# Masked attention, 16 batches on one core: the products that number batch 2's tokens move behind a query and a value product, and the tail scores wait for fewer exponentials

## The chip, the core and the metric

The kernel runs on one core of a Trainium2 chip. The metric is the device time of one execution in microseconds. TensorE (PE), VectorE (DVE), ScalarE (ACT), GpSimd (POOL) and SyncE (SP, which here only issues transfers) each work through a queue of their own in order; they meet through semaphores.

## The reference

`x` is 16 x 512 x 1024 (batch, feature, token), `cond` a 0/1 mask of 16 x 1024, `Wq` and `Wo` are 512 x 512.

```
xt = transpose(x)                         # tokens x features
q = xt @ Wq.T ; qh = q in 8 heads of 64
scores = (qh @ qh.T) / 8                  # queries = keys = values
logits = (scores * cmask + (1 - cmask) * -1e30) * rmask
out = (softmax(logits) @ qh) @ Wo.T
return x + transpose(out)
```

A token whose mask is 0 sees equal logits everywhere, so all such tokens of a batch get the mean of all values. A token whose mask is 1 attends only to tokens whose mask is 1.

## The kernel before

About half the tokens of a batch are active. The kernel numbers the active tokens of each batch (`slots`), gathers their rows (`gather`), and does the whole attention on a compact batch of A = 544, 528 or 512 tokens. Batches 2 to 15 are taken in order of their count of active tokens, which the kernel works out itself (`order`, `permute`). Rows of inactive tokens get the mean's row added (`rest`).

The work of a batch b, in the names of the code:

- `slots`: counting products on PE (L245, L247, L250: triangular and all-ones matrices against the mask), then a chain of small VectorE steps (L251 to L274) that gives each token its place and makes one-hot rows `oht`. It is done for groups of batches; for batches 2 and 3 during batch 0.
- `hot` (L319) and `index` (L328): one-hot products that place token numbers, eight small matmuls, and the copy L331 that makes `idx`, the list for the gathers (`take`, L416 on POOL).
- `xt`: transposes of the gathered rows (L507), split into two f16 parts on ACT (L465) and DVE (L466); `xt(..., 4)` is for the tail tokens beyond 512.
- `query(e, g)`: for each of four head pairs e and two column halves g, 12 f16 products (L534), copied out by ACT (L538); `qsplit` splits q into f16 parts and four transfers on SP (L562 to L565) spread them into `xx`.
- `value(e)`: products that transpose q (L588 in batch 0, L591 after it), copied by ACT (L595); `tail_copy` and `value_tail` (L604, L617) do so for the tail tokens; `range_x` is a check on magnitudes.
- `scores(b, p, u)`: 16 products (L751) for head pair p, half u, into five banks of one PSUM tile, then four exponentials on ACT (L766), in the order of places 3, 0, 1, 2. Place k takes columns 40 + 544k to 584 + 544k (for A = 544), so places 0 and 1 cover banks 0 to 2, places 2 and 3 cover banks 2 to 4. The next scores wait for all four.
- `tail_scores(b, g)`: 16 products (L698) for the scores whose keys are the tail tokens of four heads, into banks 0 and 1 of the same tile, one exponential (L702), a split on DVE (L707, L708) and four transfers on SP (L714, L715).
- `attend` (L786) and `attend_tail` (L804): the context, copied out by ACT (L809); `recip`, `norm` (L890 to L898) scale it; `project` (L908) multiplies by Wo, L914 adds x and L995 scatters the rows.

While batch b is in its scores and contexts, the steps that prepare batch b + 1 (queries, values) and b + 2 (numbers, gathers) fill PE between them. From batch 1 on, PE's order is written out by hand in `plan`. In batch 0 there is no such plan: the steps stand in a list `m` with a cost each, they are emitted between the scores in proportion to these costs, and a list scheduler decides the order of the instructions of each engine from priorities, dependencies and its own cost model. The splits of Wo (`split`, casts L183 on ACT and L184 on DVE) are inserted into `m` behind `index`, at every third place.

The scheduler sees the PSUM tile as one buffer. `other_banks` declares that an instruction does not depend on another; `self.left` holds the exponentials of the last scores in the order they were issued, that is places 3, 0, 1, 2.

Of the kernel before, what the change touches and what calls it, by code (L numbers as in the profile page):

```python
# [47 lines left out]
class Fast:  # L48
# [637 lines left out]
    def tail_scores(self, b, p):  # L686


        nc, s = self.nc, self.st[b]
        A = s["A"]  # L690
        CH = A // 2
        if True:
            pt = self.ps[:, 0:2]
            for a in range(2):
                for g in range(2):
                    for r in range(HG):
                        xx, k = s["xx"][2 * p + r // 2], r % 2
                        self.beat = nc.tensor.matmul(pt[r * CT:(r + 1) * CT, g, :CH], lhsT=xx[:, 2 * k, 512:C],  # L698
                                                     rhs=xx[:, 2 * k + a, g * CH:(g + 1) * CH],
                                                     start=(a == 0), stop=(a == 1)).ins  # L700
            t = self.sb([P, C], F32, "p", 12)[:, :A]
            self.left.append(nc.scalar.activation(t.rearrange("p (g c) -> p g c", g=2), pt[:, :, :CH], AF.Exp,  # L702
                                                  bias=s["nm"][p][:, HG:], scale=SCALE, accum_out=s["zt"][:, p:p + 1]).ins)

            hi = self.sb([P, C], F32R, "c", 4)[:, :A]
            lo = t.bitcast(F32R)
            nc.vector.tensor_copy(hi, t)  # L707
            nc.vector.tensor_tensor(lo, t, hi.bitcast(F32), ALU.subtract)  # L708

            def spread():  # L710
                s["pt"] = self.sb([P, 2, C], F32R, "pt")[:, :, :A]
                half = slice(0, DK), slice(DK, P)
                for k in range(2):
                    nc.sync.dma_start(out=s["pt"][half[k], k, :].bitcast(F32), in_=hi[half[k]].bitcast(F32))  # L714
                    nc.sync.dma_start(out=s["pt"][half[1 - k], k, :].bitcast(F32), in_=lo[half[k]].bitcast(F32))  # L715

            self.later(spread)
# [318 lines left out]
    def run(self, flag):  # L1036
# [7 lines left out]
        def xt(n):  # L1044
            return [(0.45, L(self.xt, n, c)) for c in range(4)] + [(0.25, L(self.xt, n, 4))]

        def query(n, e, g):
            u = [(1.37, L(self.query, n, e, g))]
            return u + [(0, L(self.qsplit, n, e))] if g else u

        def value(n, e):
            return [(0.45, L(self.value, n, e))]
# [91 lines left out]
        if True:  # L1144
            stack = ExitStack()
            for b in range(B + 1):
# [22 lines left out]
                if n < B:  # L1169
                    q, x, v = (lambda e, g: query(n, e, g)), xt(n)[2 if b == 0 else 0:], (lambda e: [(0.25, L(self.value, n, e))])  # L1170
                    tc, tv = ((lambda g, f=f, c=c: [(c, L(f, n, g))]) for f, c in ((self.tail_copy, 0), (self.value_tail, 0.25)))
                    rng = [(0, L(self.range_x, n, c)) for c in range(DC)]
                    ahead = b + 2 < B
                    hot, index = ([(c, L(f, b + 2))] if ahead else [] for f, c in ((self.hot, 0), (self.index, 0.2)))
                    take = [(0, L(self.gather, b + 2, j)) for j in range(5 if self.wide[b + 2] > 512 else 4)] if ahead else []
                    if self.wide[n] == 512:
                        tc = tv = lambda g: []
                    if b:
                        pre = [(0, L(self.active, *g)) for g in new[0]]
                        post = [(0.3, L(self.slots, *g)) for g in new[0]] + [(0, L(self.facts_sums, *g)) for g in new[1]]  # L1180
                        end = [(0.1, L(self.facts_end, *g)) for g in new[1]]
                        plan = {(0, 0): sums + x[:2], (0, 1): x[2:4],
                                (3, 0): rows + x[4:] + q(0, 0) + second, (3, 1): pre + q(0, 1) + carry, (4, 0): value(b, 3),
                                (5, 1): vt(b, 1) + pk(b, 1), (6, 0): post,
                                (7, 0): third + q(1, 0) + tp(b, 1), (7, 1): q(1, 1) + P_(0) + bt(b, 1), (8, 0): tc(0) + v(0) + end + rng[:2],
                                (10, 0): tv(0) + tail + q(2, 0), (11, 0): hot + rng[2:],
                                (12, 0): q(2, 1), (12, 1): index + P_(1) + v(1), (13, 0): take[:3],
                                (14, 1): rest + pk(n, 0), (16, 0): P_(2) + take[3:], (16, 1): q(3, 0) + tp(n, 0) + q(3, 1),
                                (17, 0): bt(n, 0) + v(2) + tc(1) + [(0, L(self.means, n))]}
                        carry = P_(3)  # L1190
                    else:
                        m = sums + x + pk(b, 1)
                        for g in new[0]:
                            m += [(0, permute), (0, L(self.active, *g))]
                        m += q(0, 0) + tp(b, 1) + bt(b, 1) + q(0, 1)
                        for g in new[0]:
                            m += [(0.3, L(self.slots, *g))]
                        m += hot + q(1, 0) + index + q(1, 1) + take
                        m += rng[:2] + tc(0) + v(0) + tv(0) + rng[2:] + q(2, 0) + v(1)
                        m += q(2, 1) + pk(n, 0) + tp(n, 0) + q(3, 0) + bt(n, 0)  # L1200
                        m += q(3, 1) + v(2) + tc(1) + [(0, L(self.means, n))]
                    if b == 0:
                        k = next(k for k, (c, f) in enumerate(m) if f is index[0][1])
                        for c in range(DC):
                            m.insert(k + 1 + 3 * c, (0, L(self.split, "o", c)))
                else:

                    places = [("xi", 8), ("xa", 13)]
                    come = [[L(self.late, x, j, *places[k % 2]) for j in range(5, 9)] for k, x in enumerate(rests[b])]
                    leave = [[L(self.rest, x, j) for j in range(5, 9)] for x in rests[b]]  # L1210
                    free[0] = come[0]
                    for c, l in zip(come[1:] + [[]], leave):
                        free[0] += c + l
                    plan = {(0, 0): sums, (1, 1): second, (3, 0): rows + carry + value(b, 3) + pk(b, 1),
                            (3, 1): [(0, L(self.project_means, b))], (7, 0): third + tp(b, 1) + P_(0) + bt(b, 1), (11, 0): P_(1), (13, 0): P_(2), (14, 1): [(0, self.ranges)],
                            (16, 1): P_(3)}
                if b in (1, 2):
                    plan[12, 1] += [(0, L(self.range_w, " oq"[b], c)) for c in range(DC)]
                if b == 0:
                    m = begin + m  # L1220
# [204 lines left out]
```

## Time and profile before

| | us |
|---|---|
| median of 3 runs | 1013.18 |
| lowest, highest | 1012.51, 1014.59 |
| the profiled execution | 1017.15 |
| its span (first to last instruction) | 1015.4 |

The profile is of one execution of its own, slower than the three runs. In its rows, a time at the left is the start in microseconds from the start of the span, then follow the duration, the engine, the line of the code, the operation, what is written and read, the shapes, and how many instructions were merged. A bracket at the end gives the idle time of that engine just before, and what ended it. Rows of waits read: who waited, for whom; microseconds in total, times, the longest. `ACTIVATION_READ_ACCUMULATOR` is the part of an exponential that reads the row sums out.

### The profile page before, as it was taken

The page shows a single profiled execution, that of the slowest core. Times are in us where ns is not written, and L with a number is a line of the kernel's source. Part 1 is how long each engine was busy: PE and PEld are TensorE (multiplying, and loading weights), DVE is VectorE, ACT ScalarE, POOL GpSimd, SP SyncE. Part 2 cuts the span into 40 slices and gives each one's busy share as a digit, 9 for nine tenths or more (in the row PEclk, how much of TensorE's full clock was granted, in tenths as well). Part 3 has the DMA queues.
Part 4 walks back from the last instruction along what each step waited for, and adds up shares of the span by engine and source line. Part 5 has one row for each costly group of instructions (what it writes and reads, how often), then busy time and mean ns, then how long its engine had stood idle before and what let it go on. Part 6 is the DMA issues. An engine that isn't in the chain of part 4 may idle for free. (4 is left out here: it accounts for less than half of the span.)

```text
span 1015.4 us, 23009 instructions
## 1 busy us (share of the span) xinstructions
PE 956.1 (94%) x8236; PEld 593.1 (58%) x8236; DVE 718.4 (71%) x2413; ACT 656.6 (65%) x1696; POOL 312.1 (31%) x307
## 2 busy tenths in 40 slices
PE   7788999999999999999999999999999989999887
PEld 4455666656666656666666666666666656555333
DVE  7786775767776677787777788767678866665463
ACT  5766766657667666776767677676757766555441
POOL 3101013124131322415143241515224140424752
PEclk9999999999999999999999999999999999999989
DMA  6836555557556566756657675666667564645642
GB/s 212 231 106 183 123 151 162 163 163 210 135 173 171 154 180 192 206 155 198 182 173 215 209 198 160 194 175 177 199 209 208 157 184 137 178 122 182 215 161 99
DMA packets 78793, 177.69 MB, mean 175 GB/s; under 512 B 14688, under 2 KB 20576, under 8 KB 78672
## 3 DMA queue, kind: packets, MB, share of 16 engines
q1 hardware_dynamic: 57584, 108.40, 38.5%
q0 software_dynamic: 21088, 67.75, 21.2%
q8 instruction: 67, 1.10, 0.5%
q14 instruction: 54, 0.44, 0.1%
HBM read 91.49 MB, written 33.91 MB: 123 GB/s over the span
## 5 line engine op out<-in xcount | busy, mean ns | idle before, releaser
L766 ACT ACTIVATE p<-pss,nm 128x528 f32<-128x528 f32 (+2 forms) x512 | 354.6, 703 | 108.7 <-PE pss L751 83.0
L786 PE MATMUL pss<-p,v 128*64 128x264 f32 (+2 forms) x2048 | 244.3, 391 | 0.9 <-issue 0.9
L751 PE MATMUL pss<-xx 128*128 128x86 f16 (+31 forms) x1920 | 219.8, 288 | 4.1 <-ACT c L809 2.6
L995 POOL DMA_INDIRECT y_out<-xa,idx x68 | 84.5, 1243 | 425.5 <-DVE nm L664 91.7
L786 PEld LDWEIGHTS pss<-p,v 128*64 128x64 f32 x2048 | 141.6, 137 | 88.6 <-issue 10.2
L751 PEld LDWEIGHTS <-xx 128*128 128x128 f16 (+1 forms) x1920 | 108.6, 97 | 87.6 <-issue 35.6
L534 PE MATMUL pm<-xh,wqh 128*128 128x264 f16 (+5 forms) x512 | 143.0, 279 | 7.7 <-DVE xl L466 4.2
L534 PE MATMUL pm<-xh,wql 128*128 128x264 f16 (+5 forms) x512 | 142.5, 278 | 0.0
L534 PE MATMUL pm<-xl,wqh 128*128 128x264 f16 (+5 forms) x512 | 142.4, 278 | 0.1
L534 PEld LDWEIGHTS <-wqh 128*128 128x128 f16 x1024 | 97.4, 98 | 37.0 <-issue 17.8
L416 POOL DMA_INDIRECT xa<-x_in,idx x68 | 71.6, 1054 | 129.2 <-ACT q L538 51.4
L766 ACT ACTIVATION_READ_ACCUMULATOR p<-pss,nm 128x1 f32 x512 | 105.2, 205 | 0.0
L908 PE MATMUL pm<-woh,ch 128*128 128x512 f16 x240 | 92.5, 385 | 9.4 <-ACT q L538 5.1
L538 ACT ACTIVATE q<-pm 128x264 f32<-128x264 f32 (+5 forms) x128 | 50.8, 397 | 67.1 <-PE pm L534 42.4
L908 PE MATMUL pm<-wol,ch 128*128 128x512 f16 x240 | 92.4, 385 | 0.0
L908 PE MATMUL pm<-woh,cl 128*128 128x512 f16 x240 | 92.1, 384 | 0.0
L908 PEld LDWEIGHTS <-ch 128*128 128x128 f16 x480 | 45.2, 99 | 59.8 <-issue 12.9
L995 POOL DMA_INDIRECT y_out<-xi,idx x60 | 67.7, 1128 | 38.2 <-PE pss L698 17.7
L914 DVE SCALAR_TENSOR_TENSOR xa<-pm,xa 128x512 f32<-128x512 f32 x61 | 41.6, 683 | 52.9 <-PE pm L908 52.3
L416 POOL DMA_INDIRECT xi<-x_in,idx x60 | 62.1, 1034 | 35.1 <-PE pm L534 16.5
L809 ACT COPY c<-pss 128x528 f32<-128x528 f32 (+2 forms) x64 | 38.2, 597 | 50.0 <-PE pss L804 15.2
L595 ACT COPY v<-pm 128x512 f32<-128x512 f32 x64 | 37.5, 586 | 45.8 <-PE pm L591 44.8
(241 smaller groups left out, 1504.8 us busy)
## 6 DMA issues: line engine op xcount, KB each, us to landing
xx<-hl SPq DMA_DIRECT2D x224, 136.0 KB
xm<-x_nat_in SPq DMA_DIRECT2D x56, 512.0 KB
rb<-rd SPq DMA_DIRECT2D x72, 132.0 KB
rb<-rd SPq DMA_DIRECT2D x40, 136.0 KB
pt<-c SPq DMA_DIRECT2D x36, 132.0 KB
pt<-p SPq DMA_DIRECT2D x36, 132.0 KB
ub<-ud SPq DMA_DIRECT2D x16, 256.0 KB
xx<-hl SPq DMA_DIRECT2D x32, 128.0 KB
```

What stands on the lines that cost most here:

```text
L416: dma = self.nc.gpsimd.indirect_dma_start(out=tile[:n], out_offset=None, in_=self.x, in_offset=bass.IndirectOffsetOnAxis(ap=idx, axis=0))
L534: self.beat = nc.tensor.matmul(pq, lhsT=w[:, c, e * P:(e + 1) * P], rhs=xx[:, c, cols], start=(k == 0), stop=(k == 3 * DC - 1)).ins
L538: nc.scalar.activation(s["q"][:, e, cols], pq, AF.Copy, scale=1.0 / (SX * SW))
L595: nc.scalar.copy(v, pv)
L751: m = nc.tensor.matmul(flat[:, c0:c1], lhsT=w, rhs=x, start=banks[n] not in banks[:n], stop=banks[n] not in banks[n + 1:])
L766: e = nc.scalar.activation(t, flat[:, at:at + A], AF.Exp, bias=s["nm"][p // 2][:, p % 2 * 2 + k:p % 2 * 2 + k + 1], scale=SCALE, accum_out ...
L786: mm = nc.tensor.matmul(pav[k * DK:(k + 1) * DK, g], lhsT=s["v"][p][:, i, k * DK:(k + 1) * DK], rhs=ps[k, i][:, cols], start=(i == 3), sto ...
L809: self.context_out = nc.scalar.copy(c[:, :A].rearrange("p (g c) -> p g c", g=2), pav).ins
L908: mm = nc.tensor.matmul(po[:cols.stop - cols.start], lhsT=a[:, e, cols], rhs=w[:, e, :], start=(e == 0 and k == 0), stop=(e == DC - 1 and ...
L914: return self.nc.vector.scalar_tensor_tensor(x, po, 1.0 / (SX * SW), x, ALU.mult, ALU.add).ins
L995: dma = self.nc.gpsimd.indirect_dma_start(out=self.out, out_offset=bass.IndirectOffsetOnAxis(ap=idx, axis=0), in_=x, in_offset=None)
```

## The change

Two edits. In batch 0's list, `index` and `take` of batch 2 (the products that place token numbers, and the gathers that use them) go behind the second half of query product 1, the tail copy and value product 0 of batch 1. The splits of Wo, which are inserted relative to `index`, go with them in the list. And each product of the tail scores is declared independent of `self.left[0]` and `self.left[3]`, the exponentials of places 3 and 2, whose columns lie in banks 2 to 4; it remains tied to those of places 0 and 1.

```
                         self.beat = nc.tensor.matmul(pt[r * CT:(r + 1) * CT, g, :CH], lhsT=xx[:, 2 * k, 512:C],
                                                      rhs=xx[:, 2 * k + a, g * CH:(g + 1) * CH],
                                                      start=(a == 0), stop=(a == 1)).ins
+                        self.other_banks(self.beat, self.left[0], self.left[3])
...
-                        m += hot + q(1, 0) + index + q(1, 1) + take
-                        m += rng[:2] + tc(0) + v(0) + tv(0) + rng[2:] + q(2, 0) + v(1)
+                        m += hot + q(1, 0) + q(1, 1) + tc(0) + v(0) + index + take
+                        m += rng[:2] + tv(0) + rng[2:] + q(2, 0) + v(1)
```

In the built program the number of instructions on PE, DVE, ACT and SP that do work is the same. Their order differs only in the stretch of batch 0 that the prediction walks through; in the later batches the orders are the same, and the first of each tail scores' products waits for the third of the four exponentials instead of the fourth. The line numbers here and in the prediction are those of the kernel before.

## The prediction

> **What bounds the kernel now.** I read the page first, then busy time by stretches of 100 us, then what TensorE waited for.
>
> ```profile
> span 1015.4 us, 23009 instructions
> ...
> PE 956.1 (94%) x8236; PEld 593.1 (58%) x8236; DVE 718.4 (71%) x2413; ACT 656.6 (65%) x1696; POOL 312.1 (31%) x307
> ...
> 0.00:100.00 100.00, 79.12 (x649) 49.37 (x650) 75.42 (x255) 64.80 (x168) 17.43 (x38) 0.95 0.62 182
> ...
> 600.00:700.00 100.00, 98.39 (x904) 62.52 (x901) 75.62 (x274) 69.79 (x180) 29.72 (x25) 1.00 0.64 185
> ...
> PE pm L328 <- DVE oht L274: 3.3, 1, 3.3
> ...
> PE pss L698 <- ACT p L766: 3.0, 1, 3.0
> ```
>
> PE is the bound: in the middle it is busy 98 of 100 us, so a microsecond saved on it early moves everything behind it. The first 100 us are the hole: 79 us busy, and a granted clock of 0.95. Two of the long waits there are on lines that the change touches: the index products of batch 2 (L328) wait for VectorE, and the first tail scores (L698) for an exponential. L698 has this wait once in 28 tail scores: in the others the context product ahead of them outlasts the exponentials, so the second edit is worth nothing after batch 0.
>
> An idle PE also loses its clock afterwards. These are stretches cut where the clock changes (columns: length, then PE, PEld, DVE, ACT, POOL busy, granted clock, DMA share):
>
> ```profile
> 42.21:45.62 3.41, 1.10 (x19) 0.68 (x19) 3.41 (x5) 3.41 (x11) 0.00 (x0) 1.00 0.66 186
> 45.62:49.04 3.42, 3.42 (x20) 1.63 (x20) 3.41 (x7) 2.56 (x10) 0.00 (x0) 0.50 0.70 182
> 55.86:59.28 3.42, 1.50 (x11) 0.86 (x9) 3.42 (x9) 3.38 (x10) 0.00 (x0) 1.00 0.49 154
> 59.28:62.69 3.41, 3.38 (x21) 1.79 (x20) 3.41 (x14) 3.10 (x8) 0.00 (x0) 0.50 0.02 5
> 76.34:79.76 3.42, 0.78 (x13) 0.70 (x14) 3.28 (x17) 2.63 (x7) 0.00 (x0) 1.00 0.87 202
> 79.76:83.17 3.41, 3.41 (x18) 2.06 (x16) 1.94 (x12) 0.81 (x2) 0.81 (x1) 0.50 0.95 295
> ...
> 38.80:42.21 3.41, 1.68 (x17) 0.98 (x15) 0.72 (x3) 2.47 (x7) 0.00 (x0) 1.00 1.03 258
> ```
>
> Each time PE was busy 1.50 us or less of 3.41, the next 3.41 us ran at half clock; after 1.68 us busy (the last row) they did not.
>
> **Part 1: the first tail scores.** The second edit lets them start after the third of four exponentials.
>
> ```profile
> 41.88 0.73 ACT L766 ACTIVATE p<-pss,nm 128x544 f32<-128x544 f32 x1
> ...
> 42.57 0.74 ACT L766 ACTIVATE p<-pss,nm 128x544 f32<-128x544 f32 x1
> ...
> 43.87 0.66 ACT L446 ACTIVATE xi<-xi 128x512 f32<-128x512 f32 x1
> ...
> 44.49 0.74 ACT L702 ACTIVATE p<-pss,nm 128x544 f32<-128x544 f32 x1
> ...
> 43.45 0.85 PE L698 MATMUL pss<-xx 128*32 128x272 f16 x16 [2.98 <-ACT p L766]
> 45.37 2.90 PE L751 MATMUL pss<-xx 128*128 128x472 f16 x16 [1.06 <-ACT p L702]
> ```
>
> They start 42.57 - 41.88 = 0.69 earlier, at 42.76, and end at 43.6. In the built order the tail exponential (L702) takes the place of the sum at 43.87, so it starts 44.49 - 43.87 = 0.6 earlier, and so do the next scores: 44.8 instead of 45.37. I do not expect this 0.6 to last. On ACT the built order puts a value copy and three casts of Wo (L183) ahead of the next exponentials, and on PE the transposes of the tail tokens (L507 from xt) go from a gap before the scores to behind the context product:
>
> ```profile
> 54.70 1.26 ACT L183 ACTIVATE woh<-xa 128x512 f16<-128x512 f32 x2 [0.35 <-DMA xa<-wo_in]
> 55.87 0.70 ACT L766 ACTIVATE p<-pss,nm 128x544 f32<-128x544 f32 x1
> ...
> 59.26 0.63 PE L507 MATMUL pm<-ident,xt 32*128 32x32 f32 x4
> 59.92 3.00 PE L751 MATMUL pss<-xx 128*128 128x472 f16 x16
> ...
> 64.84 0.29 PE L534 MATMUL pm<-xh,wqh 128*128 128x272 f16 x1
> ...
> 66.24 0.27 PE L651 MATMUL pm<-ident,smcol 128*128 128x128 f32 x1
> ```
>
> The four exponentials from 55.87 on would start some 0.5 later (one more cast, 1.26/2 = 0.63, and the value copy, less the 0.35 of waiting and what came earlier), near 56.4. But nothing lies between them any more, so at 0.69 each they end at 56.4 + 4 x 0.69 + 0.1, and the scores of 59.92 start near 59.3. PE idles as long before them, so the half-clock stretch at 59.28 stays; some 0.2 of the 0.6 goes into it, and the tail transposes, now uncovered, cost 0.4. At the query product of 64.84 I take 0. Bounds: 0.6 saved, or 0.6 lost if the casts wait longer for Wo.
>
> **Part 2: the slots.** Their 16 counting products (L245 to L250) come behind the tail scores and the tail's context product, no longer ahead of them.
>
> ```profile
> 72.48 0.29 PE L534 MATMUL pm<-xh,wqh 128*128 128x272 f16 x1
> ...
> 72.95 1.71 PE L751 MATMUL pss<-xx 128*128 128x472 f16 x16
> ...
> 72.11 0.15 DVE L251 COPY n<-pm 128x2 f32<-128x2 f32 x1
> ...
> 78.70 0.37 DVE L274 TENSOR_TENSOR oht<-c,tok 128x72 f16<-128x72 f16 x2
> ```
>
> The same products end by 72.48 in either order, but the query product then waits for the copy L251, which now follows the last of them: 0.15 and a handover of some 0.1. It starts at 72.75, 0.3 late. Query products follow each other at (66.24 - 64.84)/12 = 0.117; three instead of four lie ahead of the end of the scores, so these end at 74.8 instead of 72.95 + 1.71 = 74.66: 0.15 lost. VectorE's chain from L251 to L274 moves by 0.6, its end from 79.07 to 79.7.
>
> **Part 3: the stall.** L328 waits for that chain, and a query product, a value product and the next scores are queued behind it on PE.
>
> ```profile
> 78.98 0.36 PE L328 MATMUL pm<-oht,tmp 128*128 128x9 f16 x8 [3.29 <-DVE oht L274]
> ...
> 81.46 2.54 PE L751 MATMUL pss<-xx 128*128 128x472 f16 x16
> 83.92 3.89 PE L786 MATMUL pss<-p,v 128*64 128x272 f32 x32
> ...
> 88.35 0.38 PE L591 MATMUL pm<-two,xx 128*128 128x64 f16 x7
> ...
> 74.76 0.72 ACT L766 ACTIVATE p<-pss,nm 128x544 f32<-128x544 f32 x1 [1.40 <-PE pss L751]
> ...
> 77.71 0.22 ACT L766 ACTIVATION_READ_ACCUMULATOR p<-pss,nm 128x1 f32 x1
> ```
>
> Without it, 9 + 12 query products (21 x 0.117 = 2.4) and one value product (0.1) follow the scores' end, and PE is ready at 77.3. Late next are the exponentials that free the scores' banks: they took from 74.76 to 77.93, 3.17, and start 0.1 after the scores, so they end at 78.1. That is a new wait of 0.75, too short to lose the clock. The scores then take 1.71, as in the row of 72.95, and the context product starts at 79.85 instead of 83.92: 4.1 saved. Check by pieces: the wait 3.29 goes; so does the half clock (78.98 to 81.46 is 2.48 for work of 0.2 + 1.40 + 0.1, and the scores took 2.46 instead of 1.71: 1.5), and the eight index products (0.2); 0.15 and 0.75 are paid.
>
> On the clock: the Trainium skill, page "TensorE: Matmul & The Clock Gate", section "Part 1: The HAM clock gate", gives windows of 3413 ns and lets the clock fall after a window in which PE idles. The window's length agrees with the rows above; the condition does not, since 1.50 us of work in 3.41 did not keep the clock. By that rule a stall of 3.29 us alone would cost no clock.
>
> **Part 4: the moved products, and the end.** L328 now stands behind the rest of value product 0, at 79.85 + (88.35 - 83.92) + 0.3 = 84.6, 4.9 after VectorE is done with the chain: no wait, 0.2 of work. Its copy L331 waits on VectorE behind the norm of head pair 1, and L617, which is behind L328 and the scores on PE, needs L331. The gathers of batch 2 follow L331.
>
> ```profile
> 86.28 0.24 DVE L898 TENSOR_TENSOR ctl<-c,cth 128x32 f16<-128x32 f32 x1
> ...
> 8.99 1.13 POOL L416 DMA_INDIRECT xa<-x_in,idx  x1 [5.58 <-DVE later L191]
> ...
> 13.30 0.63 PE L507 MATMUL pss<-ident,xa 128*128 128x128 f32 x4 [1.56 <-DMA xa<-x_in,idx]
> ...
> 102.83 0.63 PE L507 MATMUL pm<-ident,xa 128*128 128x128 f32 x4
> ```
>
> The norm ended at 86.52 and has no reason to be later; L617 is due at 84.8 + 1.71 = 86.5. The first gather needed 13.30 - 8.99 = 4.3 from issue to use, so batch 2's lands near 91 and is read at 102.83 - 3.9 = 98.9: covered by 8 us. On SP's queue a load of x goes behind four spreads of q; its sum comes much later. From about 95 us on all engines have the old order, so the saving is carried to the end: 4.1 less 0.2, **3.9 us**.
>
> The profiled execution took 1017.15, of which 1015.4 are the span; less 3.9 that is 1013.25. It was 3.97 above the median of the three runs, 1013.18, whose work and order are the same, so I carry the difference: **1009.3 us**. About 0.2%, 2 us, is what a measurement of this kernel can tell from no change.
>
> **The rivals.** (a) The stall loses no clock in ordinary runs (the rule above): then 1.5 was never there to save, 2.4 is left, 1010.8. For it: how stretches fall on the stall may differ by run. Against it: three low stretches here, three losses.
> (b) PE is busy over 1.6 us in the stretch before 59.28 and keeps its clock: 3.00 - 1.71 = 1.3 more, 1008.0. Against it: PE waits as long as before.
> (c) The casts of Wo become the bound. They now stand ahead of the exponentials of 55.87, and SP issues Wo's loads behind four transfers of the tail exponentials (L714, L715). In the row of 54.70 a cast waited for its load, so the cover is thin. Each microsecond that the third cast passes 56.4 is lost on PE; at 2 to 4 us the gain is gone: about 1012.5. (d) The same at 4.5 us, where PE idles long enough for a further half-clock stretch (1.5): 4.5 + 1.5 - 3.9 = 2.1 slower, 1015.3; from there on the change is a loss. Against both: DMA is at 0.70 and 0.49 in those stretches, not full.
> (e) The stall is not removed but moves with L328, because VectorE's chain ends later than 84.6. Against it: 4.9 us of slack. I count it with (c).
>
> **How the numbers follow.** Forecast 0.62, (a) 0.13, (b) 0.07, (c) with (e) 0.12, (d) 0.06. Of (a), 0.08 is past 2 us. Faster by over 0.2%: 0.62 + 0.08 + 0.07 = 0.77; within 0.2%: 0.05 + 0.12 = 0.17; slower: 0.06. Range: below, (b) with the 0.6 of Part 1 and 1.2 for the spread of a median (the three runs lie 2.08 apart): 1006.2; above, (c) at 1012.6. It leaves out (d) and the ends of the others.
>
> **What would show it.** Right: no wait at L328, no half clock near 80 us, a wait of about 0.7 for the exponentials at the second scores after the slots, L698 held only by the third exponential, and the scores of 59.92 at about 59.3. Wrong: a long wait of L751 or L786 between 55 and 62 us with L183 late on ACT, or L617 waiting for L331.

## The result and the profile after

The changed kernel took 1010.68 us (median of 20 runs, 1006.18 to 1016.64), the kernel before 1016.17 in the 20 runs beside it: a ratio of 0.9935, 95% interval 0.9914 to 0.9957. The ratio is not that of the two medians, which is 0.9946. It was timed twice more: 1008.85 against 1013.91 (0.9961, 0.9929 to 0.9994) and 1008.67 against 1015.12 (0.9936, 0.9907 to 0.9966). So it is faster, by 4.0 to 6.6 us by the ratios and by 5.1 to 6.5 by the medians; the prediction's 3.9 us is a ratio of 0.9962.

Its page, and the two stretches of 100 us that were shown of before (length; PE, PEld, DVE, ACT, POOL busy; granted clock; DMA share and rate). One line was added at 701, so the lines behind it are one higher than before: L751 is now L752, L766 is L767, L786 is L787.

```profile
span 1004.5 us, 23007 instructions
...
PE 951.6 (95%) x8236; PEld 592.2 (59%) x8236; DVE 716.7 (71%) x2413; ACT 656.6 (65%) x1696; POOL 314.5 (31%) x307
...
0.00:100.00 100.00, 80.67 (x672) 51.28 (x672) 76.72 (x267) 68.60 (x179) 18.12 (x38) 0.95 0.66 188
600.00:700.00 100.00, 97.68 (x894) 62.14 (x890) 74.93 (x274) 69.32 (x180) 30.01 (x27) 1.00 0.61 177
```

The first 100 us hold 1.5 us more of PE's work, the middle is nearly as full as before (97.7 us of 100, for 98.4). The timeline of PE in the changed kernel answers the walk row by row:

```profile
42.11 0.85 PE L698 MATMUL pss<-xx 128*32 128x272 f16 x16 [2.28 <-ACT p L767]
...
59.29 1.72 PE L752 MATMUL pss<-xx 128*128 128x472 f16 x16 [1.40 <-ACT p L767]
...
71.30 0.28 PE L534 MATMUL pm<-xh,wqh 128*128 128x272 f16 x1 [0.25 <-DVE n L251]
...
76.68 1.72 PE L752 MATMUL pss<-xx 128*128 128x472 f16 x16 [0.75 <-ACT p L767]
78.33 3.89 PE L787 MATMUL pss<-p,v 128*64 128x272 f32 x32
...
82.97 0.35 PE L328 MATMUL pm<-oht,tmp 128*128 128x9 f16 x8
83.18 1.70 PE L752 MATMUL pss<-xx 128*128 128x472 f16 x16
...
93.44 0.30 PE L651 MATMUL pm<-ident,smcol 128*128 128x128 f32 x1 [2.58 <-DVE smcol L645]
```

L328 has no wait, the exponentials hold PE for 0.75 us, the copy L251 for 0.25. These three were forecast. The last row was not: the transpose of the peaks (L651) now waits 2.58 us. In before the same row reads, with the gathers and the query's copy that belong to it:

```profile
82.36 0.95 POOL L416 DMA_INDIRECT xa<-x_in,idx  x1 [46.86 <-ACT q L538]
...
87.55 0.87 POOL L416 DMA_INDIRECT xt<-x_in,idx  x1 [0.30 <-issue]
...
96.28 0.42 ACT L538 ACTIVATE q<-pm 128x274 f32<-128x274 f32 x1
...
97.82 0.30 PE L651 MATMUL pm<-ident,smcol 128*128 128x128 f32 x1 [0.46 <-DVE smcol L645]
```

and in the changed kernel:

```profile
84.63 0.95 POOL L416 DMA_INDIRECT xa<-x_in,idx  x1 [49.76 <-ACT v L595]
...
89.84 1.22 POOL L416 DMA_INDIRECT xt<-x_in,idx  x1 [0.30 <-issue]
...
88.80 0.28 PE L534 MATMUL pm<-xh,wqh 128*128 128x274 f16 x1
89.15 1.71 PE L752 MATMUL pss<-xx 128*128 128x472 f16 x16
...
91.98 0.40 ACT L538 ACTIVATE q<-pm 128x274 f32<-128x274 f32 x1 [1.34 <-PE pss L752]
```

PE's rows end its query product at about 89.3 and the scores behind it at 90.9, yet ScalarE, which has nothing else to do from 90.64 on, copies that product only at 91.98. The fifth of five gathers that GpSimd issues back to back ends at 89.84 + 1.22 = 91.06. VectorE's chain to `smcol` stands behind that copy in VectorE's order, and L651 needs the chain.

To follow the saving, this table gives the start of the same instructions of PE in each profile, less that in before (us; negative is earlier). The heads are before's times: a query product, the second scores after the slots, two later scores, and L651 between them. From 111 us on the orders are those of before. The profile of e12 is from another chip than the others.

| profile | 64.84 | 72.95 | 95.65 | L651, 97.82 | 111.37 |
|---|---|---|---|---|---|
| changed | -1.56 | -1.43 | -6.50 | -4.38 | -1.95 |
| changed, second (e4) | -0.99 | -0.92 | -5.99 | -3.73 | -3.65 |
| changed, third (e10) | -0.19 | -0.06 | -5.14 | -3.03 | -0.58 |
| before again (e11) | 1.49 | 1.48 | 1.41 | 1.42 | 1.44 |
| list alone (e1) | 0.59 | 0.58 | -4.60 | -2.66 | -2.59 |
| ties alone (e2) | -0.02 | 0.04 | 0.68 | 3.15 | 1.21 |
| products in the wait (e3) | -0.57 | 0.11 | -0.84 | -0.84 | -0.83 |
| gathers twice (e5) | 1.16 | 1.23 | -3.84 | -0.25 | 4.33 |
| plain transfers (e6) | -0.08 | -0.02 | -5.09 | -5.09 | -2.84 |
| slots early (e7) | 0.82 | 1.16 | -2.50 | -2.49 | -2.49 |
| slots early, ties (e8) | 1.38 | 1.52 | -1.60 | -1.60 | -1.60 |
| gathers split (e9) | -0.90 | -0.77 | -5.84 | -5.21 | 0.80 |
| index first (e12) | -0.43 | -0.37 | -5.40 | -5.40 | 0.60 |

Between 72.95 and 95.65 every profile with the list's edit (the changed kernel's three, e1, e5, e6, e9, e12) gains 5.0 to 5.2 us. At L651 the changed kernel gives back 2.1 to 2.3 of them.

### The profile page after: what moved, and what is told of

The parts are those of the page before. It is cut to its first block, busy times and chain, and to the rows that moved or that the text cites. A ratio compares the mean times of both kernels' runs of the same rounds, so it can differ in the third digit from the quotient of the medians.

```text
span 1004.5 us, 23007 instructions
## 1 busy us (share of the span) xinstructions
PE 951.6 (95%) x8236; PEld 592.2 (59%) x8236; DVE 716.7 (71%) x2413; ACT 656.6 (65%) x1696; POOL 314.5 (31%) x307
## 5 line engine op out<-in xcount | busy, mean ns | idle before, releaser
L767 ACT ACTIVATE p<-pss,nm 128x528 f32<-128x528 f32 (+2 forms) x512 | 354.7, 704 | 103.6 <-PE pss L752 75.6
L787 PE MATMUL pss<-p,v 128*64 128x264 f32 (+2 forms) x2048 | 245.9, 393 | 0.9 <-issue 0.9
L752 PE MATMUL pss<-xx 128*128 128x86 f16 (+31 forms) x1920 | 216.1, 285 | 4.5 <-ACT p L767 2.2
L787 PEld LDWEIGHTS pss<-p,v 128*64 128x64 f32 x2048 | 142.4, 138 | 89.1 <-issue 11.1
L752 PEld LDWEIGHTS <-xx 128*128 128x128 f16 (+1 forms) x1920 | 107.3, 96 | 85.9 <-issue 33.3
L416 POOL DMA_INDIRECT xa<-x_in,idx x68 | 74.2, 1092 | 125.4 <-ACT v L595 49.8
L767 ACT ACTIVATION_READ_ACCUMULATOR p<-pss,nm 128x1 f32 x512 | 105.3, 206 | 0.0
L846 DVE COPY rr<-pm 10x128 f32<-10x128 f32 x49 | 13.4, 274 | 74.6 <-PE pm L841 68.0
```

Source lines behind the costliest of these rows:

```text
L416: dma = self.nc.gpsimd.indirect_dma_start(out=tile[:n], out_offset=None, in_=self.x, in_offset=bass.IndirectOffsetOnAxis(ap=idx, axis=0))
L752: m = nc.tensor.matmul(flat[:, c0:c1], lhsT=w, rhs=x, start=banks[n] not in banks[:n], stop=banks[n] not in banks[n + 1:])
L767: e = nc.scalar.activation(t, flat[:, at:at + A], AF.Exp, bias=s["nm"][p // 2][:, p % 2 * 2 + k:p % 2 * 2 + k + 1], scale=SCALE, accum_out ...
L787: mm = nc.tensor.matmul(pav[k * DK:(k + 1) * DK, g], lhsT=s["v"][p][:, i, k * DK:(k + 1) * DK], rhs=ps[k, i][:, cols], start=(i == 3), sto ...
L846: self.spot_reads += [nc.vector.tensor_copy(rr, pt[:10]).ins] * spot
```

## The experiments

The expectations name these theories. Theory 1: the gain is the stall at L328 and the half-clock window behind it. Theory 2: the freed tail scores bring much of it. Theory 3: stops of PE that differ from run to run make the rest. Theory A came with the first profiles: while GpSimd issues a chain of gathers, the other engines learn late that PE has finished.

**The first edit alone (e1).**

```
-                        m += hot + q(1, 0) + index + q(1, 1) + take
-                        m += rng[:2] + tc(0) + v(0) + tv(0) + rng[2:] + q(2, 0) + v(1)
+                        m += hot + q(1, 0) + q(1, 1) + tc(0) + v(0) + index + take
+                        m += rng[:2] + tv(0) + rng[2:] + q(2, 0) + v(1)
```

> Only the first edit: the list puts the index products of batch 2 behind the second query product and the first value product; tail scores keep all their ties. Theory 1 (the gain is the stall of 3.29 us at L328 and the half-clock window behind it): PE's order up to 75 us is that of before, no wait stands at L328, the scores that began at 81.46 begin 4.5 to 5 us earlier, and the time falls by 3.9 to 4.5 us, ratio 0.9956 to 0.9962. Theory 2 (the freed tail scores bring a good part of it, by other orders around 43 to 73 us): under 3 us. Theory 3 (stops of PE that differ from run to run make the rest of the measured 6.6 us): the two profiles differ by several us behind 90 us, the medians by about 4.

Measured: ratio 0.9969 (0.9935 to 1.0003). In the table 5.18 us are gained from 72.95 to 95.65, 1.94 lost at L651. PE's timeline:

```profile
84.86 0.35 PE L328 MATMUL pm<-oht,tmp 128*128 128x9 f16 x8
...
95.16 0.30 PE L651 MATMUL pm<-ident,smcol 128*128 128x128 f32 x1 [2.40 <-DVE smcol L645]
```

No wait at L328, and the same new wait at L651. The list's edit alone makes the gain of this stretch, against Theory 2. By the times alone Theory 2 can't be excluded: 0.9969 misses the 0.9956 to 0.9962 expected, and the changed kernel came out between 0.9935 and 0.9961.

**The second edit alone (e2).**

```
+                        self.other_banks(self.beat, self.left[0], self.left[3])
```

> Only the second edit: tail scores tied to two exponentials. The scheduler of PE's order, which is free in batch 0, then places the index products behind the scores, the context and the tail context by itself, since they are due late. Theory 1: L328 finds its operands ready here too, the stall goes without the list's edit, and the time falls by 3.5 to 4.5 us, as much as with the other edit alone; the two do not add up. Theory 2: the second edit brings 2 to 3 us by itself and the first one 4, so that this run gains 2 to 3 and the whole change 6.6. If the edit were worth nothing behind batch 0 and nothing at L328, the ratio would be 1.000.

Measured: 0.9991 (0.9959 to 1.0023). PE's timeline:

```profile
78.16 1.99 PE L752 MATMUL pss<-xx 128*128 128x472 f16 x16 [2.18 <-ACT p L767]
...
85.86 0.36 PE L328 MATMUL pm<-oht,tmp 128*128 128x9 f16 x8
...
94.92 0.19 PE L591 MATMUL pm<-two,xx 128*128 128x64 f16 x1 [3.63 <-DMA xx<-hl]
```

A stretch of the same profile (length; PE, PEld, DVE, ACT, POOL busy; granted clock; DMA share and rate):

```profile
79.45:82.86 3.41, 3.41 (x21) 1.67 (x18) 3.34 (x16) 2.67 (x7) 0.00 (x0) 0.50 0.94 270
```

A miss: the stall at L328 is gone here too, as expected, but nothing came of it. PE waits 2.18 us for the exponentials instead of 0.75, with the half-clock window behind that as in before, and 3.63 for the spread of q. Removing the stall is worth something only if what stands behind it on PE is ready; here query product 1's second half comes behind L328 and its consumers are late. L651 waits 2.62 us here too, though the copy ahead of it is on time: part of the value product stands behind the scores in this order. So such a wait can come from an order as well, and of the runs below e5, e6 and e9 keep PE's order and change the gathers alone.

**Products in the wait (e3).** The kernel before; ten products of ones ahead of the index products of batch 2.

```
+        wt = self.pm([P, 4, P]) if b == 2 else None
+        [nc.tensor.matmul(wt, lhsT=self.on16, rhs=self.on16.unsqueeze(1).broadcast_to([P, 4, P]),
+                          start=True, stop=True) for _ in range(10 if b == 2 else 0)]
```

> The kernel before with ten products of ones (128x512, into a tile that nobody reads) ahead of the index products of batch 2, in the 3.29 us in which PE waits there: the wait for DVE stays, the clock should not be lost. Added work: ten products of 512 columns, about 2.2 us at full clock, inside the wait. Theory 1 with a clock lost in ordinary runs: the index products start where they did (near 79), the window behind them runs at full clock, and the time falls by 1.2 to 1.6 us, ratio 0.9985. Rival (a) (ordinary runs lose no clock there): 0.0 us, ratio 1.000. If the products end late they cost up to 0.3.

```profile
75.64 2.32 PE L326 MATMUL pm<-on 128*128 128x512 f16 x10
...
79.10 0.36 PE L328 MATMUL pm<-oht,tmp 128*128 128x9 f16 x8 [1.14 <-ACT xm L446]
80.74 1.71 PE L751 MATMUL pss<-xx 128*128 128x472 f16 x16
```

L328 starts at 79.10 instead of 78.98, as meant. (Its row names an ACT operation as the end of the wait; VectorE's last one-hot rows, L274, start at 78.81.) The scores behind it start 0.72 earlier (80.74 for 81.46) and take 1.71 instead of 2.54, so the next ones, of 88.82, start 1.54 earlier, or 1.65 counted from 72.95, where this run is 0.11 late: that is the price of the half-clock window, 1.5 in the prediction. Of it 0.70 goes again in the stretch to 95.65, where the copies of the context are waited for. The time's ratio, 0.9952 (0.9915 to 0.9989), is more than this stretch explains (0.9985 was expected).

**The changed kernel again (e4, e10) and before again (e11).**

> The changed kernel itself, beside its two halves on the same chip. Theory 1: 4 us, ratio 0.996, the same as each half alone within 1 us. Theory 2: the sum of the halves, 6 to 7 us, ratio 0.9935. Theory 3: between 4 and 7 with a wide interval, and the stops of PE behind 90 us lie elsewhere than in the profile at hand.

> The changed kernel again, for the size. The stretch from 73 to 95 us gained 5.07 us in each of its profiles, and 2.1 to 2.3 of it went at L651; with a scatter of 0.9 us up to 65 us. If that is all: 2.8 us, ratio 0.9972. The prediction's 3.9: 0.9961. The first measurement, 6.6: 0.9935. The profile is expected to show 5.0 to 5.1 and 2.0 to 2.4 us again.

> The kernel before, with a line that does nothing: the same instructions. It shows what a difference of two kernels of this length is worth: ratio 1.000, with an interval of about 0.0035 to both sides. Its profile is a second look at before: the stall of 3.3 us at L328 and the half-clock window behind it should be there again; the half-clock windows and waits behind 200 us should not all lie where they did.

Measured: 0.9961 (0.9929 to 0.9994) and 0.9936 (0.9907 to 0.9966) for the changed kernel, 0.9981 (0.9949 to 1.0013) for the repeat of before, whose instructions are the same: about 2 us between two samples of one kernel are chance. The three profiles of the changed kernel gain 5.07, 5.07 and 5.08 us from 72.95 to 95.65 and lose 2.12, 2.26 and 2.11 at L651. The repeat of before has its stall again:

```profile
80.47 0.36 PE L328 MATMUL pm<-oht,tmp 128*128 128x9 f16 x8 [3.30 <-DVE oht L274]
...
99.23 0.30 PE L651 MATMUL pm<-ident,smcol 128*128 128x128 f32 x1 [0.47 <-DVE smcol L645]
```

**The gathers twice (e5).** In the changed kernel, each gather into `xa` of batch 2 comes a second time, into a tile that is not read.

```
         if j < 4:
+            if b == 2: self.rows(s["idx"][:, j:j + 1], self.sb([P, D], F32, "xi", 8))
             s["xa"].append(...)
```

> The changed kernel with each of the four row gathers of batch 2 that fill xa issued twice, the first time into a tile that nobody reads. All engines but GpSimd keep their orders. In the changed kernel TensorE stood 2.58 and 2.73 us at L651 although all that its chain needs had run; ScalarE there waited for TensorE's products that had ended 2 us before, and was released about 1 us behind the last of five gathers issued back to back. Theory A (while GpSimd issues a chain of gathers, other engines learn late that TensorE has finished): the chain grows by four gathers of 1.25 us, and the wait at L651, or waits near it that replace it, grows by 4 to 5 us in all. Theory B (the stop at L651 has to do with the load of the scores or the query's own chain): the wait stays at 2.4 to 2.8 us.

GpSimd, ScalarE and PE of this kernel (its lines are one higher again: L539 is the query's copy, L652 the transpose):

```profile
87.30 0.95 POOL L416 DMA_INDIRECT xi<-x_in,idx  x1 [51.48 <-ACT v L596]
...
97.77 1.09 POOL L416 DMA_INDIRECT xt<-x_in,idx  x1 [0.30 <-issue]
...
96.08 0.40 ACT L539 ACTIVATE q<-pm 128x274 f32<-128x274 f32 x1 [2.87 <-remote]
...
97.57 0.30 PE L652 MATMUL pm<-ident,smcol 128*128 128x128 f32 x1 [4.06 <-DVE q L542]
```

(`remote` is a releaser that the profile does not tell.) The query product of this copy ends at 91.97 in PE's rows, so the copy is 4.1 us late, where it is 2.7 late in the changed kernel. It is released while the chain still runs, which ends at 98.86: the news is late during the chain, but does not always wait for its end. Up to L651 this profile loses 3.59 us of its lead at 95.65, the changed kernel 2.1 to 2.3. Up to 111.37 it loses 8.17 us, the changed kernel 4.55, 2.34 and 4.56, so the four gathers cost 3.6 to 5.8 there (4 to 5 were expected), part of it as half-clock windows, of which this profile has three from 98.18 on and the changed kernel's have two, none and two. Its time was taken only once (1021.23 us), and nothing is read from it.

**Plain transfers for the gathers (e6).** The changed kernel, with transfers on SP's queue that read other rows of x than the list names, so the output is not the reference's. The code is shortened.

```
-            s["xa"].append(self.rows(s["idx"][:, j:j + 1], ...))
+            d = self.nc.sync.dma_start(out=t[:n], in_=self.x[j * P:j * P + n])
```

> The changed kernel with the five gathers of batch 2 replaced by five plain transfers of as many rows and bytes on SP's queue, behind the same index product (other rows of x are read than the masks ask for). Orders of TensorE, VectorE and ScalarE stay. Theory A (the chain of gathers on GpSimd delays the news that TensorE has finished): the wait at L651 falls from 2.6 to about 0.5, the lead over before that stood at 6.0 at the scores of 95.65 is kept to 5.5 or more at those of 111.37, and the time is 1.5 to 2.3 us below the changed kernel's, ratio to before 0.994. Theory B: the wait at L651 stays near 2.6 and the ratio at 0.996.

```profile
92.73 0.30 PE L657 MATMUL pm<-ident,smcol 128*128 128x128 f32 x1 [0.47 <-DVE smcol L651]
...
98.26 0.19 PE L597 MATMUL pm<-two,xx 128*128 128x64 f16 x1 [1.91 <-DMA xx<-hl]
```

The wait at the transpose (here L657) is back at 0.47, as Theory A expected, with the orders of the changed kernel on PE, VectorE and ScalarE. The lead of 5.09 is whole at L651, and then 2.25 of it go, 1.91 to a wait for the spread of q. The time, 1.0024 (0.9990 to 1.0058), missed the expected 0.994: what was won at L651 did not reach the end, and where behind 111 us it went is not known.

**The slots early (e7), and with the freed tail scores (e8).** Before, with the slots ahead of query product 0; e8 adds the second edit.

```
-                        m += q(0, 0) + tp(b, 1) + bt(b, 1) + q(0, 1)
                         for g in new[0]:
                             m += [(0.3, L(self.slots, *g))]
+                        m += q(0, 0) + tp(b, 1) + bt(b, 1) + q(0, 1)
```

> The kernel before with the slots of batches 2 and 3 computed ahead of the first query product of batch 1, and neither edit of the change: the one-hot products of VectorE are then ready some 6 us sooner and the index products find them where they stood. Theory 1: no wait at L328, 0.75 us for the exponentials instead, no half clock behind it: 4.1 us gained by the scores of 88.82. Theory A: the gathers start 3 to 4 us sooner in time, at the same place in TensorE's order as in before, so that little is given back at L651 (0.5 us of wait as in before): ratio 0.995 to 0.996. If the early slots hold up the first query product of batch 1 or the shift at L651 near 66, 0.5 to 1 us of it is lost.

> The early slots of the run before this one and the change's second edit, but not its first: tail scores tied to two exponentials, the index products in their old place. Theory 1 with Theory A: the 0.8 us that the profiles show for the freed tail scores up to 64.84, 4.1 us at L328, nothing given back at L651: 5 us, ratio 0.9945 to 0.9955, better than the changed kernel by about 1.4 us. If the wait at L651 came with the freed tail scores instead of the place of the gathers, it stands here at 2.4 us and the ratio is that of the changed kernel, 0.996.

Both missed: 0.9991 (0.9956 to 1.0025) and 1.0007 (0.9974 to 1.0039). PE and ScalarE of e7:

```profile
76.24 0.35 PE L328 MATMUL pm<-oht,tmp 128*128 128x9 f16 x8
77.38 0.28 PE L534 MATMUL pm<-xh,wqh 128*128 128x274 f16 x1 [0.79 <-DVE idx L331]
...
95.33 0.30 PE L651 MATMUL pm<-ident,smcol 128*128 128x128 f32 x1 [0.47 <-DVE smcol L645]
...
87.27 0.61 ACT L809 COPY c<-pss 128x544 f32<-128x544 f32 x1 [3.15 <-PE pm L591]
```

No stall at L328 and, with the chain of gathers from 79.70 to 86.02, no long wait at L651 either; the context's copy is late, released 1.25 us behind the chain (in before 1.34, at 89.76). But the early slots cost 1.4 us between the scores of 59.92 (0.23 early) and of 72.95 (1.16 late), and a new wait for the copy L331 takes 0.79. In e8 the wait at L651 is 0.47 too, so the freed tail scores did not bring it.

**The gathers split (e9).** In the changed kernel, three gathers stay; two wait for the end of the last query product of batch 1.

```
+                        m += hot + q(1, 0) + q(1, 1) + tc(0) + v(0) + index + take[:3]
...
+                        m += q(2, 1) + pk(n, 0) + tp(n, 0) + q(3, 0) + bt(n, 0) + take[3:]
```

> The changed kernel with the chain of five gathers cut in two: three stay behind the index products, the fourth and the fifth wait for the end of the last query product of batch 1 (101 us in before, 97.4 in the changed kernel), ahead of the context product of 3.9 us in which TensorE waits for little. All engines but GpSimd keep their orders; the rows are read first at 106.8 and 109.6. Theory A: the first chain ends near 89, before the query product whose news came late, so the wait at L651 falls from 2.6 to about 0.5 us and 2.0 to 2.2 us are gained by 94 us; the second chain may cost 0 to 1.5 us between 98 and 104. Ratio to before 0.993 to 0.996, 1 to 2 us below the changed kernel. Theory B (the stop has nothing to do with the gathers): the wait at L651 stays at 2.4 to 2.8.

```profile
92.61 0.30 PE L651 MATMUL pm<-ident,smcol 128*128 128x128 f32 x1 [1.09 <-DVE smcol L645]
...
100.23 0.21 PE L591 MATMUL pm<-two,xx 128*128 128x64 f16 x1 [4.00 <-DMA xx<-hl]
```

The first part of the chain ends at 88.95 and the wait falls from 2.6 to 1.09 (0.5 expected), so 1.5 us are won. Then PE waits 4.00 for the spread of q, against 1.23 in before. Ratio 0.9964 (0.9929 to 0.9999): no better than the changed kernel, where 1 to 2 us better were expected.

**The index products ahead of the context (e12).** The changed kernel, with a priority that puts them behind the second scores after the slots.

```
+            with self.tc.high_priority(offset=250 if b == 2 else 0):
                 self.pe = self.spotted(nc.tensor.matmul(pi, ...)).ins
```

> The changed kernel with a higher priority for the eight index products of batch 2: the scheduler then places them behind the second scores after the slots and ahead of the context product (in the changed kernel: behind that context, near 83.5). VectorE's chain ends near 78.7, so they find their operands after at most 0.3 us. Theory A: the gathers start some 3 us sooner and their chain ends near 88, before the query product whose news was late; the wait at L651 falls from 2.6 to about 0.5 us, the lead at the scores of 95.65 stays near 5 or loses up to 0.9 to the context's copies, which now see the chain, as they do in before. Net 1.2 to 2.1 us below the changed kernel: ratio 0.992 to 0.995. Theory B: the wait at L651 stays at 2.4 to 2.8 and the ratio at 0.9945.

PE and SP of e12:

```profile
79.39 0.36 PE L328 MATMUL pm<-oht,tmp 128*128 128x9 f16 x8
...
92.42 0.30 PE L651 MATMUL pm<-ident,smcol 128*128 128x128 f32 x1 [0.47 <-DVE smcol L645]
...
101.25 0.21 PE L591 MATMUL pm<-two,xx 128*128 128x64 f16 x1 [5.20 <-DMA xx<-hl]
...
93.40 0.37 SPq L455 DMA_DIRECT2D xm<-x_nat_in  x1
93.87 0.48 SPq L562 DMA_DIRECT2D xx<-hl  x1
```

With the chain done at 87.86 the wait at L651 is 0.47, as Theory A has it, and all 5.03 us are there at L651. Then 6.0 are lost to the scores of 111.37, 5.20 of them in one wait for the spread of q. SP issues that spread 0.47 us behind a load of x of 512 KB on the same queue; in the second profile of the changed kernel (e4) the load went at 92.55 and the spread at 94.67, 2.1 us later, and PE waited 0.16. In e9 the spread goes 0.62 us behind that load, and PE waits 4.00. That the load holds up the spread is argued from these three; no run moved the load. The time missed the expected 0.992 to 0.995. This run was on a chip where before takes 986.44; the ratio there, 0.9992 (0.9978 to 1.0006), is of e12 to before, and the changed kernel was not run on that chip.

## Why the prediction was right, and where it was not

**The direction and the mechanism** were right. The stall at L328 goes by the list's edit (e1), with the half-clock window behind it, whose price e3 measured by itself: 1.54 us for the 1.5 of the walk. Rival (a) falls: the window near 80 us is in both profiles of before and in none of the changed kernel. The time alone would not tell this: 1010.68 is nearer to rival (a)'s 1010.8 than to the forecast's 1009.3. That it lies 1.4 us from the forecast is in part luck, since the kernel before took 1016.17 beside it and not the 1013.18 that the forecast started from.

**Part 1** walked a wait of 2.29 at L698 (2.28 found) and the scores of 59.92 at 59.3. They are at 59.29, but this is luck: the profile is 0.62 us early already at the first scores, at 32.29, and counted from there the three profiles of the changed kernel stand at -0.01, -1.32 and 0.01 here. At the query product of 64.84 the walk took 0, with 0.6 to both sides. Measured from the first scores, at 32.29, the three profiles of the changed kernel and e9 are 0.8 to 0.9 early there, e5, e6 and e12 with the same orders up to there 1.2, 0.7 and 0.2 late, and four profiles with the old tail scores lie from 0.1 early to 1.4 late. The bounds were too narrow. The clock is the larger part of it: between 32 and 65 us every one of the early profiles, before and e3 hold two half-clock windows, and e1, e5, e6, e11 and e12 three. With two windows the changed order is ahead by 0.8 to 0.9, which the walk did not have. Rival (b) came true in part: the scores near 59.3 ran at full clock (1.72 us) in the first profile, e9 and e10, and lost it (3.10) in e4. It is a matter of the run, not of the edit, since e3 keeps it too, without the edit. But each profile that kept it lost a second window near 47 us instead, as the first does here, so (b)'s 1.3 us were not won:

```profile
46.59:50.01 3.42, 3.42 (x21) 1.69 (x19) 2.98 (x11) 2.41 (x8) 0.00 (x0) 0.50 0.83 185
```

**Part 2**: 0.3 late at the query product, 0.25 found; 0.15 lost by the next scores, 0.07 to 0.13 found.

**Part 3**: a wait of 0.75 for the exponentials, 0.75 found; the context product at 79.85, 79.70 in e10, whose lead at 72.95 is only 0.06; 4.1 saved, 4.16 found in e4 (from 83.92 to 78.84, less its lead of 0.92). Another 0.9 was won up to 95.65, which the walk did not have: in before the context's copy is released only at 89.76, 1.34 behind the end of the chain of gathers, and the scores of 88.82, which wait for it, took 2.36 us up to 91.18; in the changed kernel 1.70.

**Part 4 is the step that failed.** It asked of the gathers only when their rows land, found 8 us of cover, gave back 0.2 for the work of L328 and let the saving be carried to the end from 95 us on. But the chain of five gathers, some 6.4 us long, is moved past PE's work together with `index`: it now lies over the query product whose copy feeds L651, and that costs 2.1 to 2.3 us for which the walk had no term. e5 (chain longer, more lost), e6 (no chain, 0.47) and e9 (chain shorter, 1.09), all with the changed kernel's orders on PE, VectorE and ScalarE, show the cause; e12 (chain earlier, 0.47) agrees. Nor have all engines the old order from 95 us on: VectorE's differs up to 104.8. Behind it, the first and the third profile lose two half-clock windows more. These are the first profile's stretches cut at the windows (columns as above):

```profile
90.97:94.38 3.41, 0.94 (x8) 0.84 (x9) 2.11 (x9) 0.40 (x1) 0.09 (x1) 1.00 0.66 204
94.38:97.79 3.41, 3.16 (x17) 2.24 (x15) 1.15 (x9) 2.01 (x7) 0.00 (x0) 0.50 0.88 267
97.79:101.20 3.41, 1.62 (x18) 1.20 (x16) 2.56 (x10) 3.04 (x8) 0.00 (x0) 1.00 0.01 3
101.21:104.62 3.41, 3.13 (x14) 1.94 (x16) 2.11 (x4) 0.60 (x1) 0.00 (x0) 0.50 0.72 163
```

**The sum.** At 111.37 the three profiles of the changed kernel stand at -2.06 on average, the two of before at 0.72: 2.8 us, in place of 3.9. The runs say 4.0 to 6.6. Behind 111 us the instructions and orders are the same, and yet that stretch takes 894 to 904 us in these five profiles, so no single profile tells what comes of 2.8 us there. The leads at 111.37 do not even order the ratios: e6 and e7, early by 2.84 and 2.49, came out at 1.0024 and 0.9991, and e9, late by 0.80, at 0.9964. So the stretch's gain is shown, and that it makes the whole of the measured 4.0 to 6.6 is not. Much of the scatter is the clock: in the 28 runs of before beside e9 to e11, the time and the time lost to half clock (one less the granted clock, times the time) have a correlation of 0.82, with a slope of 1.1. Beside e4, before lost 15.4 us so and the changed kernel 11.1; beside e10, 15.9 and 12.4, where the repeat of before lost 14.3. One window, 1.7 us, is the one at L328; the rest of that difference has no place in the traces that I could find. Whether it belongs to the change or to chance is left open.

Of the other rivals, (c) and (d) did not happen, since the scores of 59.92, counted from 32.29, came at most 0.5 us later than in before (e5), and (e) did not either: in e4 VectorE's chain ended at 78.7, 4.8 us before L328.

## What to carry to other kernels

A moved step takes its transfers' issue with it: ask not only when the rows land but which engine's news, copies and queue the issue itself lies over at the new place. Each stall that is taken out of a chain uncovers the next one (here the exponentials, the peaks' transpose, the spread of q behind a load), so follow the lead instruction by instruction up to where the orders are the same again, in more than one profile. And with a scatter of 4 us in 1000, time the kernel before against itself before believing a second microsecond.

## What the runs showed of the hardware

News of PE's work comes late while GpSimd issues gathers back to back. With no gather near, an idle ScalarE copies a query product 0.04 us after the end of PE's last row of it (99.55 in before). With the chain over it the copy came 2.7 us late (first profile), 2.8 (e4), 2.65 (e10), 2.5 (e1) and 4.1 (e5). In the first four it was released 0.9 to 1.4 us behind the end of the chain, in e5 while the chain still ran. Since the ends of PE's rows are modelled, it can't be told whether PE was late or its signal. The Trainium skill, page "Perfetto Trace Analysis", section "DMA Instruction — SWDGE (GPSIMD)", says that such a row ends when the last descriptor is written, and not when the data are moved. The traces agree in that the gather of 8.99 in before has a row of 1.13 us, and PE waited for its rows until 13.30. No run here shows whether the writing of descriptors or the moving of data holds up the news.

The clock's windows lie on a grid that runs by itself: in the profile of before the half-clock stretches at 45.62, 59.28, 79.76 and 219.70 are whole multiples of 3.413 us apart, in each other profile too, and the grid's place differs from run to run. So the same idle time loses a window in one run and none in another. PE's busy time in a window does not tell sharply which one loses the clock: 1.62 us did not keep it (the row of 97.79), while 1.60 did in the same profile, and in e4 1.78 did not and 1.53 did. These are the first profile's stretch and the two of e4:

```profile
56.83:60.24 3.41, 1.60 (x13) 1.01 (x13) 3.41 (x12) 3.41 (x10) 0.00 (x0) 1.00 0.16 53
...
54.67:58.08 3.41, 1.78 (x17) 1.08 (x11) 3.41 (x8) 3.41 (x9) 0.00 (x0) 1.00 0.45 162
...
92.22:95.63 3.41, 1.53 (x13) 1.34 (x14) 1.98 (x7) 0.40 (x1) 0.00 (x0) 1.00 0.72 234
```

Chips differ: before took 986.44 us on one and 1011.98 to 1016.17 on the others, with a scatter (standard deviation) of 1.6 us there and of about 4 elsewhere. The granted clock, with 9.7 us lost there against 15, explains a fifth of it; the rest is open.
